# Output sums and two softplus steps on GpSimd in a selective scan, and a later issue of two small products in a mixture of experts

## The chip, the cores and the metric

One core of a Trainium2 chip runs the whole program in one launch. The metric is the device time in microseconds (us) of the program, as the median of several executions. The engines are TensorE (PE; its weight loads are PEld), VectorE (DVE), ScalarE (ACT), GpSimd (POOL) and SyncE (SP), which issues most DMAs. Each works through its own queue in order, and they wait for one another through semaphores.

## The reference, cut to what matters

The network has four layers on an image of 128 channels and 48 x 48 pixels, four images. Layer 0 is a selective scan in four directions, layer 1 a deformable convolution, layer 2 a linear attention and a mixture of experts, layer 3 a causal attention and a mixture of experts. The change is in layer 0 and in both mixtures. Of layer 0:

```python
xs = jnp.stack([x_hw, x_wh, x_hw[..., ::-1], x_wh[..., ::-1]], axis=1)
x_dbl = jnp.einsum('bkdl,kcd->bkcl', xs, x_proj_w)
dts, Bs, Cs = jnp.split(x_dbl, [R, R + N], axis=2)
delta = jax.nn.softplus(jnp.einsum('bkrl,kdr->bkdl', dts, dt_w) + dt_b[None, :, :, None])
A = -jnp.exp(A_logs)
out_y = _selective_scan(xs, delta, A, Bs, Cs, Ds)
inv = out_y[:, 2:4, :, ::-1]
y = out_y[:, 0] + inv[:, 0] + wh(out_y[:, 1]) + wh(inv[:, 1])
```

The scan is, for each channel and each of N = 16 states, h(t) = h(t-1) * exp(delta(t) * A) + delta(t) * u(t) * B(t), and the output is the sum over the states of h * C. Of the experts:

```python
logits = jnp.einsum('bsd,ed->bse', x, gate_w) + gate_b
probs = jax.nn.softmax(logits, axis=1)
vals, idx = jax.lax.top_k(probs.transpose(0, 2, 1), K)
```

where x is the layer-normed state: each of 64 experts takes its 8 best of 2304 tokens of an image, and its input is their sum, weighted by the probabilities.

## The kernel before, in words

**Layer 0** works on pieces. A piece is one image, one direction k and one third (768 positions, CH) of the sequence: 4 x 4 x 3 = 48 pieces, in the order of directions 0, 2, 1, 3 (PIECES). The 256 inner channels are two halves of 128 partitions, d = 0 and 1. A piece takes 16 steps, one for each state n, so there are 768 steps. What a step issues, and in which order, is written out by hand (STEPS, with a lag in steps for some parts):

```python
STEPS = """
pa s10 d1 s00 row t0 t2 fill t1 b0 e0 fill s11 s01 spread pb col b2 b1 fill e1 keep d0 fill
a2
"""
```

Every engine but SP takes its instructions in exactly this order. The parts: `pa` (times_b, L572) is POOL's product of du and B for the last 256 positions of both halves, one step ahead. `s10`, `s00`, `s11`, `s01` are the scans on DVE (L605), halves 1 and 0, first 512 positions and then 256; the first read their input b from PSUM, the second read what `pa` wrote in SBUF. `d0`, `d1` are exp(delta * A) on ACT (L557). `row` (L552) is a DMA on SP that spreads a row of B over the partitions for `pa`. `spread` (L539) is a select on POOL that lays column B out as diagonal blocks dB, three steps ahead, into two buffers; `e0`, `e1` (fill_b, L582) are PE's products of dB and du into the two PSUM banks b, one step ahead. `t0`, `t2`, `t1` transpose h on PE (L619), ACT scales by C (L629), `b0`, `b1` transpose back and sum in PSUM (L651); for the middle 256 positions `a2` sums on DVE instead (L643). `keep` (L612) saves the last state on POOL. So `spread` of a step waits for `e1` of the same step, which frees its buffer, and the next step's first scan waits for that `e1` too.

`col` is, in steps 3 and 4, `collect` of the piece before: for direction 0 it writes u * D + ys to y (L694, always on DVE), for the other three it adds ys to y (L703), for directions 1 and 3 with the two spatial axes exchanged. After the last one of an image, y goes to memory (SP), from where the tail of that image fetches it.

Each `fill` takes the next items of two lanes, spread evenly over the fills: the lane `next` prepares the next piece (31 items over 48 fills), the lane `image` does the tail of the image before or the head of the next. The items of `next` that matter are, in order: `log(0)`, `carry`, `less(0)`, `log(1)`, `total(0)`, `inputs(0)`, `less(1)`, `total(1)`, `inputs(1)`, and then the transposes of du on PE. They end the softplus, log(1 + e) + max(., 0), with a correction for rounding: `rest` (DVE, L459) finds the correction, `log` is ACT, `less` (L467) subtracts the correction from the logarithm, `total` (L470) adds that to delta, `inputs` (L474) multiplies delta and u into du. All are 128 x 768 for one half d.

**The experts** (`_experts`, once for layer 2 and once for layer 3) work on two pairs of images, q = 0 and 1. `shifted(b)` (L2091) makes -mean * rstd of image b on DVE, for all 18 token tiles at once; `gates(q)` normalises tokens (L2112 and L2110: one tile of three each on ACT, DVE and POOL), transposes them (L2127) and projects them on the experts (L2138); `select(q)` finds the eight largest of each expert on DVE (MAX8, L2160) and goes on from there. ACT's share of the normalising uses `shift`. The last of rstd of image 3 is a power on POOL, of layer 2's end (L1228) or of layer 3's (L2555). Then 16 groups of four experts are computed, whose weights SP loads into four buffers.

Of the kernel before, what the change touches and what calls it, by code (L numbers as in the profile page):

```python
# [24 lines left out]
NB = 4  # L25
# [102 lines left out]
def _layer0(ctx, env, dr, io, table, offs):  # L128
# [7 lines left out]
    nc, tc, ident = env.nc, env.tc, env.ident  # L136
# [255 lines left out]
    def prepare(x, before_it):  # L392

        k, at = x.k, x.at
        t = {}
# [68 lines left out]
            nc.scalar.activation(x.du[:, d, :], x.du[:, d, :], AF.Ln)  # L464

        def less(d):
            nc.vector.tensor_sub(x.du[:, d, :], x.du[:, d, :], t["e"][:, d, :])  # L467

        def total(d):
            nc.vector.tensor_add(x.delta[:, d, :], x.delta[:, d, :], x.du[:, d, :])  # L470

        def inputs(d):

# [17 lines left out]
        def carry():  # L491
# [23 lines left out]
            lambda: log(0),  # L515
            carry,
            lambda: less(0),
            lambda: log(1),
            lambda: total(0),
            lambda: inputs(0),  # L520
            lambda: less(1),
            lambda: total(1),
            lambda: inputs(1),
        ] + [
# [158 lines left out]
    def collect(x, d):  # L683

        src = x.ys[:, d, :]
        if x.k % 2:
            w0 = x.c * (CH // HW)
            dst = y[:, d, :].rearrange("p (h w) -> p w h", w=HW)
            dst = dst[:, w0 : w0 + CH // HW, :]
            src = src.rearrange("p (w h) -> p w h", h=HW)  # L690
        else:
            dst = y[:, d, x.at : x.at + CH]
        if x.k == 0:
            nc.vector.scalar_tensor_tensor(  # L694
                dst,
                u_hw[:, d, x.at : x.at + CH],
                dsum[:, d : d + 1],
                src,
                op0=ALU.mult,
                op1=ALU.add,  # L700
            )
        else:
            nc.vector.tensor_add(dst, dst, src)  # L703
        if (x.k, x.c, x.ci) == PIECES[-1] and d == ND - 1:
            nc.sync.dma_start(x.im.y, y)

# [271 lines left out]
    with tc.manual_schedule(engines=ORDERED):  # L978
# [20 lines left out]
        for g in range(len(pieces) * NS - min(lags.values())):  # L999
            i, n = divmod(g, NS)  # L1000
            b, p = divmod(i, NPI)
# [27 lines left out]
        for d in range(ND):  # L1029
            collect(pieces[-1], d)  # L1030
# [1014 lines left out]
def experts(env, io, pre, T, known, out=None):  # L2045


    with ExitStack() as ctx:
        _experts(ctx, env, io, pre, T, known, out)


def _experts(ctx, env, io, pre, T, known, final):


    nc, tc, ident = env.nc, env.tc, env.ident
# [7 lines left out]
    def psum(*shape):  # L2063
        return ps.tile(list(shape), F32, name="psum", tag="ps")
# [23 lines left out]
    def shifted(b):  # L2088
        mv, rstd = known[b]
        shift = sp.tile([P, NT], F32, name="shift", bufs=NB)  # L2090
        nc.vector.scalar_tensor_tensor(  # L2091
            shift, mv[:, :, 0], -1.0, rstd, op0=ALU.mult, op1=ALU.mult
        )
        image[b].update(mv=mv, rstd=rstd, shift=shift)

    def gates(q):

        t = {}

        def norm(j):  # L2100
            for r in range(2):
                b = 2 * q + r
                m = image[b]
                for g in range(G3):
                    i = j * G3 + g
                    src, dst = T[:, b * NT + i, :], xh[:, b * NT + i, :]
                    scale = m["rstd"][:, i : i + 1]
                    if g == 0:
                        shift = m["shift"][:, i : i + 1]
                        nc.scalar.activation(dst, src, AF.Identity, bias=shift, scale=scale)  # L2110
                        continue
                    (nc.vector if g == 1 else nc.gpsimd).tensor_scalar(  # L2112
                        dst,
                        src,
                        m["mv"][:, i, 0:1],
                        scale,
                        op0=ALU.subtract,
                        op1=ALU.mult,
                    )

        def turn(j):
            t[j] = []
            for r in range(2):
                pt = psum(P, BLK)
                for g in range(G3):
                    i = (2 * q + r) * NT + j * G3 + g
                    nc.tensor.transpose(pt[:, bass.ts(g, P)], xh[:, i, :], ident)  # L2127
                xT = sp.tile([P, BLK], F32, name=f"xT{r}")
                if r:
                    nc.scalar.copy(xT, pt)  # L2130
                else:
                    nc.vector.tensor_copy(xT, pt)
                t[j].append(xT)

        def project(j):
            pg = psum(P, BLK)
            for r, xT in enumerate(t.pop(j)):
                nc.tensor.matmul(  # L2138
                    pg[r * NE : (r + 1) * NE, :], gate_w, xT, start=True, stop=True
                )  # L2140
            nc.scalar.activation(G[:, q, bass.ts(j, BLK)], pg, AF.Identity, bias=gate_b)

        def step(j):
            if j + 1 < NBLK:
                norm(j + 1)
            if 0 <= j < NBLK:
                turn(j)
            if j > 0:
                project(j - 1)

        return [lambda j=j: step(j) for j in range(-1, NBLK + 1)]
# [120 lines left out]
    def turn_T(tT, n):  # L2272

        pt = psum(P, BLK)
        for g in range(G3):
            nc.tensor.transpose(pt[:, bass.ts(g, P)], T[:, n * G3 + g, :], ident)
        dst = tT[:, bass.ts(n, BLK)]
        if n % 2:
            nc.scalar.copy(dst, pt)
        else:  # L2280
            nc.vector.tensor_copy(dst, pt)

    def both(a, b):

        n = max(len(a), len(b))
        for i in range(n):
            for s in (a, b):
                for x in s[i * len(s) // n : (i + 1) * len(s) // n]:
                    x()

    with tc.manual_schedule(engines=ORDERED):
        for b in range(NB):
            shifted(b)
        both(gates(0), [])
        both(gates(1), select(0))
        both(select(1), [])
        tT = None
        if final is not None:
            tT = cp.tile([P, NB * L], F32, name="tT", tag="xh")
        last, turns = None, 0  # L2300
        for n in range(NE // EG + 1):
            new = Group(n * EG) if n < NE // EG else None
            if new:
                new.hidden()
            if last:
                last.output()
            if new:
                new.turned()
            if last:
                last.keep()  # L2310
            while tT is not None and turns * (NE // EG) < NB * NBLK * n:
                turn_T(tT, turns)
                turns += 1
            last = new
        for q in range(npair):
            pt = psum(P, C)
            both_oT = oT[:, 2 * q : 2 * q + 2, :].rearrange("p b e -> p (b e)")
            nc.tensor.transpose(pt, both_oT, ident)
            o = sp.tile([P, C], F32, name="o")
            nc.scalar.copy(o, pt)  # L2320

            halves = [slice(r * NE, (r + 1) * NE) for r in range(2)]
            for j in range(NBLK):
                pp = [psum(P, BLK) for r in range(2)]
                if final is None:
                    for g in range(G3):
                        for r, half in enumerate(halves):
                            nc.tensor.matmul(
                                pp[r][:, bass.ts(g, P)],
                                G[half, q, bass.ts(j * G3 + g, P)],  # L2330
                                o[half, :],
                                start=True,
                                stop=True,
                            )
                    for r in range(2):
                        i0 = (2 * q + r) * NT + j * G3
                        dst = T[:, i0 : i0 + G3, :].rearrange("p g c -> p (g c)")
                        nc.vector.tensor_add(dst, dst, pp[r])
                    continue
                for r, half in enumerate(halves):  # L2340
                    nc.tensor.matmul(
                        pp[r], o[half, :], G[half, q, bass.ts(j, BLK)], start=True, stop=True
                    )
                for r in range(2):
                    b = 2 * q + r
                    res = sp.tile([P, BLK], F32, name="res", tag=f"xT{r}")
                    nc.vector.tensor_add(res, tT[:, bass.ts(b * NBLK + j, BLK)], pp[r])
                    nc.sync.dma_start(final[b][:, bass.ts(j, BLK)], res)
# [516 lines left out]
```

## Time and profile before

| what | value |
|---|---|
| median of 3 runs | 10886.33 us (10877.05 to 10887.75) |
| the profiled execution | 10882.38 us |
| its span, first to last instruction | 10880.7 us |
| mean granted TensorE clock | 0.951 |
| layer 0, about | 145 to 4700 us of the span |
| deformable convolution, linear attention | 4700 to 9195 us |
| experts of layer 2 | 9195 to 9390 us |
| layer 3's attention | 9390 to 10707 us |
| experts of layer 3 | 10707 to 10880 us |

The page gives, for each engine, its busy time and share of the span, then costly groups of instructions: line, engine, operation, what is written and read, shape and count, then busy time in us, the mean of one in ns, and the engine's idle time just before them with what ended most of it. The timeline gives instructions in order: start and duration in us, engine, line, operation, and in brackets the idle time of the engine before it and what ended it. Neighbours of one kind are merged (x2), and one instruction's start can lie some 0.08 us before the end of the one ahead of it.

### The profile page before, as it was taken

Reading aid. Unit: us, or ns where it says so; the run is one execution under the profiler, and the core shown is the slowest. Engines: PE = TensorE matmul, PEld = TensorE weight load, DVE = VectorE, ACT = ScalarE, POOL = GpSimd, SP = SyncE. Lnnn points to the kernel's source line nnn. Section 1 sums busy time; section 2 is a strip of 40 time slices with the busy share of each in tenths; the row PEclk is TensorE's granted clock in tenths of the full one; section 3 lists DMA queues with packets and bytes.
Section 4 is the critical chain, followed back from the end, with each engine's and each line's share of the span. In section 5 each row is a group of like instructions: output and inputs, shape, how many; then the busy total and the mean of one; then the engine's idle time right before and its main releaser. Section 6 shows DMA issues by size and latency. Waiting matters only on the chain. (4 is left out here: it accounts for less than half of the span.)

```text
span 10880.7 us, 211759 instructions
## 1 busy us (share of the span) xinstructions
PE 9607.1 (88%) x82560; PEld 7581.2 (70%) x82560; DVE 8293.1 (76%) x15739; ACT 6673.8 (61%) x11320; POOL 4186.2 (38%) x4773
## 2 busy tenths in 40 slices
PE   7999889988998899857778999999999997799887
PEld 6789777977797777645666878877778875333333
DVE  5998899889988999755677888877888876455553
ACT  5777777777777777612234777767777775233333
POOL 2433343334333434356655444434444443000001
PEclk9999999999999999867888999999999999899999
DMA  4222223222322232255544000000000001200004
GB/s 138 75 81 70 81 83 97 70 77 85 96 73 79 83 92 76 86 175 166 155 138 121 27 25 27 28 21 26 25 27 27 24 28 50 98 7 8 8 9 145
DMA packets 424637, 763.45 MB, mean 70 GB/s; under 512 B 85428, under 2 KB 246983, under 8 KB 422487
## 3 DMA queue, kind: packets, MB, share of 16 engines
q1 hardware_dynamic: 368266, 576.68, 16.5%
q0 software_dynamic: 51840, 169.91, 5.5%
q8 instruction: 657, 10.76, 0.4%
q10 hardware_dynamic: 3532, 3.30, 0.1%
q14 instruction: 342, 2.79, 0.1%
HBM read 608.94 MB, written 74.69 MB: 63 GB/s over the span
## 5 line engine op out<-in xcount | busy, mean ns | idle before, releaser
L629 ACT ACTIVATE hs<-ps,bct 128x256 f32<-128x256 f32 x3072 | 1285.8, 473 | 775.5 <-PE yp L651 411.1
L582 PE MATMUL b<-dB,duT 128*128 128x128 f32 x12288 | 1694.9, 282 | 65.2 <-DVE h L605 53.5
L582 PEld LDWEIGHTS b<-dB,duT 128*128 128x128 f32 x12288 | 1531.0, 195 | 183.7 <-DVE h L605 79.5
L539 POOL TENSOR_SCALAR_AFFINE_SELECT dB<-bct 128x512 f32<-128x512 f32 x768 | 575.8, 750 | 2666.0 <-PE b L582 2569.4
L557 ACT ACTIVATE dA<-delta,l_Al 128x768 f32<-128x768 f32 x1536 | 1406.8, 939 | 161.5 <-DVE h L605 159.6
L619 PE MATMUL ps<-ident,h 128*128 128x128 f32 x9216 | 1249.8, 277 | 203.8 <-DVE acc L643 141.6
L605 DVE TENSOR_TENSOR_SCAN h<-dA,carry,b 128x512 f32<-128x512 f32 x1024 | 1252.7, 1264 | 218.8 <-PE b L582 187.8
L619 PEld LDWEIGHTS ps<-ident,h 128*128 128x128 f32 x9216 | 1033.8, 142 | 393.8 <-DVE acc L643 185.3
L605 DVE TENSOR_TENSOR_SCAN h<-dA,h 128x256 f32<-128x256 f32 x1536 | 1074.8, 741 | 0.0
L572 POOL TENSOR_TENSOR h<-du,rB 128x512 f32<-128x512 f32 x768 | 1003.3, 1306 | 49.0 <-DVE du L474 6.6
L651 PE MATMUL yp<-ident,hs 128*128 128x128 f32 x6144 | 950.8, 277 | 59.2 <-ACT hs L629 46.7
L2580 ACT ACTIVATE pT<-scT 128x768 f32<-128x768 f32 (+2 forms) x504 | 378.1, 750 | 728.4 <-PE scT L2572 728.3
L651 PEld LDWEIGHTS yp<-ident,hs 128*128 128x128 f32 x6144 | 728.9, 143 | 105.9 <-ACT hs L629 71.1
L605 DVE TENSOR_TENSOR_SCAN h<-dA,b 128x512 f32<-128x512 f32 x512 | 595.2, 1204 | 121.6 <-PE b L582 108.5
L1868 ACT ACTIVATE gl<-psum,l_cols 128x384 f32<-128x384 f32 x768 | 438.1, 581 | 317.6 <-PE psum L1867 288.4
L643 DVE SCALAR_TENSOR_TENSOR acc<-ps,bct,acc 128x256 f32<-128x256 f32 x1440 | 617.9, 470 | 1.5 <-PE ps L619 1.5
L1341 POOL DMA_INDIRECT g<-table,idx x476 | 520.7, 1094 | 252.2 <-issue 80.2
L1876 PEld LDWEIGHTS psum<-w,gl 128*128 128x128 f32 x4608 | 567.7, 193 | 50.1 <-ACT gl L1868 0.6
L1876 PE MATMUL psum<-w,gl 128*128 128x128 f32 x4608 | 594.5, 277 | 0.5 <-ACT gl L1868 0.5
L1867 PE MATMUL psum<-uT,w 128*128 128x384 f32 x1536 | 577.2, 498 | 0.8 <-ACT gl L1868 0.5
L1526 POOL TENSOR_TENSOR wk<-wk,wkr 128x384 f32<-128x384 f32 x171 | 172.2, 1007 | 1054.3 <-DVE wk L1525 1036.6
L2512 DVE TENSOR_REDUCE mx<-sc 128x4 f32<-128x2048 f32 (+2 forms) x200 | 396.6, 1983 | 213.8 <-PE sc L2501 211.1
(426 smaller groups left out, 20388.7 us busy)
## 6 DMA issues: line engine op xcount, KB each, us to landing
rB<-rows SPq DMA_DIRECT2D x768, 384.0 KB
w<-f_w SPq DMA_DIRECT2D x64, 1024.0 KB
wkr<-wk SPq DMA_DIRECT2D x384, 96.0 KB
wqr<-wq SPq DMA_DIRECT2D x384, 96.0 KB
table<-zero SPq DMA_DIRECT2D x162, 128.0 KB
table<-tok SPq DMA_DIRECT2D x16, 1152.0 KB
yd<-y SPq DMA_DIRECT2D x4, 2304.0 KB
sums<-raw SPq DMA_DIRECT2D x192, 48.0 KB
```

The costliest lines, as they stand in the source:

```text
L539: nc.gpsimd.affine_select(out=x.dB[n], in_=x.bc[:, m0 : m0 + CT // P, n : n + 1].to_broadcast([P, CT // P, P]), pattern=[[0, CT // P], [1, ...
L557: nc.scalar.activation(dA, x.delta[:, d, :], AF.Exp, scale=A[:, d, x.k, n : n + 1])
L572: engine.tensor_mul(h[:, :, lo:hi], x.du[:, :, lo:hi], rb)
L582: nc.tensor.matmul(bt[:, bass.ts(m, P)], x.duT[d][:, m, :], x.dB[n][:, m0 + m, :], start=True, stop=True,)
L605: nc.vector.tensor_tensor_scan(h, da, src, initial=first, op0=ALU.mult, op1=ALU.add)
L619: nc.tensor.transpose(tt[:, m, bass.ts(d, P)], x.h[n][:, d, bass.ts(2 * q + m, P)], ident)
L629: nc.scalar.activation(hs, tt[:, m, :], AF.Copy, scale=c)
L643: nc.vector.scalar_tensor_tensor(acc[:, m, :], tt[:, m, :], c, acc[:, m, :], op0=ALU.mult, op1=ALU.add)
L651: nc.tensor.matmul(yp[:, q, (2 * d + m) * P : (2 * d + m + 1) * P], hs[:, bass.ts(d, P)], ident, is_transpose=True, start=n == 0 and m == ...
L1341: nc.gpsimd.indirect_dma_start(out=g, out_offset=None, in_=table, in_offset=bass.IndirectOffsetOnAxis(ap=self.idx[:, k : k + 1], axis=0),)
L1867: nc.tensor.matmul(pg, y.w["w1"][:, bass.ts(f, P)], t["uT"], start=True, stop=True)
L1876: nc.tensor.matmul(pp[:, g, :], t["gl"][:, f, bass.ts(g, P)], y.w["w2"][:, f, :], start=f == 0, stop=f == DFF // P - 1,)
```

## The change

Three lines move from DVE to POOL, and one loop of the experts is split:

```diff
         def less(d):
-            nc.vector.tensor_sub(x.du[:, d, :], x.du[:, d, :], t["e"][:, d, :])
+            nc.gpsimd.tensor_sub(x.du[:, d, :], x.du[:, d, :], t["e"][:, d, :])

         def total(d):
-            nc.vector.tensor_add(x.delta[:, d, :], x.delta[:, d, :], x.du[:, d, :])
+            nc.gpsimd.tensor_add(x.delta[:, d, :], x.delta[:, d, :], x.du[:, d, :])
...
         else:
-            nc.vector.tensor_add(dst, dst, src)
+            nc.gpsimd.tensor_add(dst, dst, src)
...
     with tc.manual_schedule(engines=ORDERED):
-        for b in range(NB):
+        for b in range(2):
             shifted(b)
         both(gates(0), [])
+        for b in range(2, NB):
+            shifted(b)
         both(gates(1), select(0))
         both(select(1), [])
```

`less` and `total` are issued 96 times each, the addition of `collect` 72 times (three directions of four), all 128 x 768. Their places in the order of issue stay. `inputs`, between them on DVE, now reads what POOL wrote. In the experts, `shifted` of images 2 and 3 is issued behind the whole of `gates(0)`.

## The prediction

> **What bounds the kernel now.** I read the page first, then busy times by stretch, then the trace of layer 0 row by row, since 264 of the moved instructions lie there.
>
> From the page and from the busy times by stretch (span, then PE, PEld, DVE, ACT, POOL busy, clock, DMA share, GB/s):
>
> ```profile
> PE 9607.1 (88%) x82560; PEld 7581.2 (70%) x82560; DVE 8293.1 (76%) x15739; ACT 6673.8 (61%) x11320; POOL 4186.2 (38%) x4773
> ```
> ```profile
> 2500.00:3000.00 500.00, 447.80 (x3471) 386.58 (x3470) 465.16 (x680) 373.96 (x670) 203.03 (x242) 0.98 0.31 91
> 4700.00:9195.00 4495.00, 3998.31 (x41332) 3322.89 (x41333) 3372.99 (x8632) 2772.46 (x4461) 2229.78 (x2372) 0.94 0.20 61
> ```
>
> In layer 0 (about 145 to 4545 us) DVE and PE are both nine tenths busy and POOL four tenths: on averages, moving work from DVE to POOL looks free. So I cut the trace into steps, each beginning with the first of four scans (L605); 16 steps make a piece, 48 pieces the layer. A step without extra work takes 4.41 us, all of it DVE's: two long scans 2.36, two short ones 1.29, the two adds of L643 0.77. By the mean over pieces, steps 0 to 2 are PE's (DVE idles 0.8 to 1.5 us before the scans that follow) and steps 3 to 12 are DVE's (PE idles 0.65 us in step 8, 1.94 in step 9). In 35 of the 47 pieces prepared inside this loop `less(0)` stands in step 7, `total(0)` and `inputs(0)` side by side at the end of step 8, `less(1)` in the middle and `total(1)` at the end of step 9, `inputs(1)` in the middle of step 10; in 9 of the other 12 `total(0)` and `inputs(0)` stand side by side as well, later. Mean lengths of steps 7 to 10: 5.89, 6.47, 6.28, 5.64 us. Here is one step 8, DVE and then POOL (start, duration, idle time before it and who ended it):
>
> ```profile
> 1457.78 2.44 DVE L605 TENSOR_TENSOR_SCAN h<-dA,carry,b 128x512 f32<-128x512 f32 x2
> 1460.14 1.36 DVE L605 TENSOR_TENSOR_SCAN h<-dA,h 128x256 f32<-128x256 f32 x2
> 1461.43 0.93 DVE L470 TENSOR_TENSOR delta<-delta,du 128x768 f32<-128x768 f32 x1
> 1462.39 1.27 DVE L474 TENSOR_TENSOR du<-delta,u_hw 128x768 f32<-128x768 f32 x1
> 1463.59 0.86 DVE L643 SCALAR_TENSOR_TENSOR acc<-ps,bct,acc 128x256 f32<-128x256 f32 x2
> ```
> ```profile
> 1457.55 1.28 POOL L572 TENSOR_TENSOR h<-du,rB 128x512 f32<-128x512 f32 x1
> 1462.01 0.84 POOL L539 TENSOR_SCALAR_AFFINE_SELECT dB<-bct 128x512 f32<-128x512 f32 x1 [3.18 <-PE b L582]
> 1462.82 1.96 POOL L572 TENSOR_TENSOR h<-du,rB 128x512 f32<-128x512 f32 x1
> ```
>
> The reader is to see two things. POOL's `spread` (L539) waits for the last `fill_b` of PE in each step; over the pieces it starts 4.02 us (median) into step 8, when DVE is past its scans. Whatever POOL is given after `spread` starts no earlier. And two instructions that overlap get longer: the select took 0.84 instead of 0.64 while L470 ran, L474 1.27 instead of 0.95 while the select ran, L572 1.96 instead of 1.28 while L474 ran. Each waits about as long as the other still runs. It holds for short scans too (POOL, then DVE, which took 1.36 in the rows above):
>
> ```profile
> 1394.64 1.55 POOL L358 COPY u_wh<-u_hw 128x768 f32<-128x768 f32 x1
> ```
> ```profile
> 1395.02 2.36 DVE L605 TENSOR_TENSOR_SCAN h<-dA,h 128x256 f32<-128x256 f32 x2
> ```
>
> The long scans, which read b in PSUM, run at 2.44 beside L572 all through the layer. [...]
>
> **The change, step by step.** What DVE loses:
>
> ```profile
> L470 DVE TENSOR_TENSOR delta<-delta,du 128x768 f32<-128x768 f32 x96 | 100.3, 1045 | 0.4
> L703 DVE TENSOR_TENSOR y<-y,ys 128x768 f32<-128x768 f32 x72 | 96.1, 1336 | 3.6 <-ACT ys L678 3.6
> L467 DVE TENSOR_TENSOR du<-du,e 128x768 f32<-128x768 f32 x96 | 93.9, 978 | 0.0
> ```
>
> 290 us of DVE. POOL's price for 768 elements is not in the trace: it lies between 1.00 us for 384 (L1526) and 5.32 for 2304 (L1311); with 1.28 for 512 (L572) the line through the last two gives 1.28 + 256 x 2.25 ns = 1.86 us, which I take. The strided sums (two of three) may cost more: POOL's strided copy of 768 is 1.55, so I take 2.0. [...]
>
> *Step 7:* `less(0)` goes: -0.85 us (its start-to-start time; nothing, if PE bounds the step: the late tenth of `spread` is 6.29 there). On POOL it ends some 1.5 to 2 us into step 8, beside long scans; but the L572 behind it then meets the short scans, which the wait in step 8 hides.
>
> *Step 8:* `inputs(0)` on DVE now waits for `total(0)`, which stands behind `spread` in POOL's queue. 4.02 + 0.64 + 1.86 = 6.52 us. What POOL does next (`keep`, 0.26, in two pieces of three, else L572, 1.31: mean 0.61) has SBUF first: 7.13. Then `inputs(0)` 0.87 and L643 0.77: 8.77 us, against 6.47. +2.3. Without the 0.61 it is +1.7; with a `spread` at its late tenth (5.54) it is +3.2 or more. Behind `inputs(0)` on DVE stand L643 and the next scans, and PE waits for both.
>
> *Step 9:* `less(1)` and `total(1)` go: 6.28 - 0.85 - 0.95 = 4.48. But `spread` starts 4.66 us into step 9, so PE delivers no sooner; I take 4.8: -1.5 (bounds -1.8 and -1.0).
>
> *Step 10:* `total(1)` ends 4.66 + 0.64 + 1.86 = 7.16 us after the start of step 9, 2.36 into step 10, just when DVE comes to `inputs(1)`; the instruction behind it on POOL is first again (0.6) and an L572 then meets a short scan (0.3): +0.9 (bounds 0 and +1.3).
>
> Sum for a piece: -0.85 + 2.3 - 1.5 + 0.9 = +0.85; x 48 = **+41 us** (bounds -46 and +168: from -0.95 to +3.5 a piece, all of one side at once, which I don't expect).
>
> *Output sums:* 36 pieces, one each in steps 3 and 4. Step 3: DVE loses 1.26 of 5.96, but PE has 5.37 us of matmuls there at their usual spacing and `spread` starts at 4.94: -0.95. On POOL the sum then runs to 2.6 us into step 4 and L572 to 4.1, over the short scans due at 2.36: they lose 1.5, the second sum saves 1.26, +0.2. In step 5 L572 ends at 2.8: +0.4. Sum -0.35 x 36 = **-13 us** (bounds -91, both sums saved whole, and +22, nothing saved in step 3).
>
> *Ends of images:* PE waited 19.6 us in three times for y to come back (L729), DVE's last two sums take 2.84 us. Sums on POOL end 1.5 us later each time: **+5 us** (bounds 0 and +10). No SP queue is passed: y's DMA follows the same sum.
>
> *Experts.* `shifted` of images 2 and 3 goes behind `gates(0)`: two DVE instructions of 0.18 us, no DMA. In layer 2's experts the one for image 3 holds up DVE:
>
> ```profile
> 9214.71 12.47 POOL L2112 TENSOR_SCALAR xh<-T,known 128x128 f32<-128x128 f32 x16
> 9227.14 0.89 POOL L1228 TENSOR_TENSOR known<-known,half 128x3 f32<-128x3 f32 x1
> 9228.05 0.18 DVE L2091 SCALAR_TENSOR_TENSOR shift<-known 128x18 f32<-128x18 f32 x1 [17.43 <-POOL known L1228]
> ```
>
> Afterwards `gates(0)` (12.3 us long, 9228.05 to 9240.37) runs from 9210.6, its POOL part ready by 9219; the wait stays but comes behind it, so the first MAX8 can start at 9228.3 instead of 9240.37: **-12 us**, if POOL's order stays (bounds 0, if that square root slips behind, and -17.4). Weight loads follow the groups, which start as much earlier. In layer 3's experts the wait is 3.16 us, but POOL starts its normalising only after it: **-1 us** (bounds 0 and -3.2).
>
> Total 41 - 13 + 5 - 13 = **+20 us**. The profiled execution was 10882.4 us (span 10880.7), 4 below the median of the three runs, 10886.3; on the median, 10906.
>
> **Rivals.** *Faster:* POOL and DVE hinder each other less than assumed, so that step 8 costs +1.7, step 10 nothing: -0.65 a piece, -31; the sums bring -1.2 x 36 = -43; with -13 and +3, -84: 10802. For it: long scans and L643 are over half of a step and are not hindered. Against it: the overlaps above, and PE's load in steps 3 and 4. It decides where the contention costs under 0.2 us a moved instruction. *Much slower:* one mechanism, POOL's queue. DVE's delayed step lets PE start its chain late, `spread` slips, and `total` with it, in both halves: `inputs(1)` stalls about 1.3 us more. +2.2 a piece, +106, sums 0, +5 - 13: 10984. It decides once `spread` in step 9 begins over 5 us into it. For it: the late tenth of `spread` there is 6.61. Against it: PE is idle 1.94 us in that step. *The experts' edit does nothing* (POOL's square root slips with it): 10918.
>
> **Numbers.** Forecast case, 10865 to 10950: 0.48. Faster, 10780 to 10865: 0.28. Much slower, 10950 to 11030: 0.19. Experts void, near 10918: 0.05. The range 10815 to 10985 leaves out a third of the second and half of the third. Faster by over 0.2% (about what a measurement of this kernel can tell, 22 us: below 10865) 0.28; within it 0.24, the lower half of the forecast case; above 10908 0.48, its upper half, the third and the fourth.
>
> **What would show it.** Step 8 near 8.8 us, with L474 waiting for POOL L470 about 2.5 us, 40-odd times; L474 in step 10 with little wait; step 9 near 4.8; L605's short scans longer in the mean than 741 ns; L467 and L470 on POOL near 1.9 us. The first MAX8 of layer 2's experts 12 us nearer to the last adds of its layer. Wrong if DVE's wait before L474 is under 1 us, or if steps 3 and 4 lose their full 1.26.

## The result, and the profile after

Measured beside the kernel before, the changed kernel takes 10994.25 us (median of 4 runs, 10976.29 to 11003.36) against 10887.04 (4 runs, 10877.05 to 10891.32). The ratio is 1.0094, 95% interval 1.0081 to 1.0106: slower by 107 us. The forecast, 10906, had the sign right and a fifth of the size, and the time lies 9 us above the range.

The profiled execution took 10976.29 us, with a span of 10974.6: 94 us longer than before's. Cut at the same events, the two traces differ as follows:

| stretch | before, us | after, us | difference |
|---|---|---|---|
| up to the first scan | 145.6 | 149.0 | +3.4 |
| first scan to the last step of layer 0 | 4391.4 | 4488.4 | +97.0 |
| rest of layer 0, to the first gather | 158.2 | 161.4 | +3.2 |
| deformable convolution to the last T of layer 2 | 4513.5 | 4506.5 | -7.0 |
| last T to the first MAX8 of layer 2's experts | 31.7 | 19.7 | -12.0 |
| first MAX8 to layer 3's first | 1483.8 | 1494.9 | +11.1 |
| layer 3's first MAX8 to the end | 156.5 | 154.7 | -1.8 |

The loss is in layer 0. The -7.0 and the +11.1 lie where no instruction is changed but layer 3's two `shifted`; in the traces of the other kernels below the stretch of the +11.1 is 1486 to 1497 us long, with the experts' edit and without it, so that before's, the shortest of all, is the odd one. The page of after (busy times; then busy us, mean ns and idle time of three groups):

```profile
PE 9642.2 (88%) x82560; PEld 7622.3 (69%) x82560; DVE 8181.9 (75%) x15475; ACT 6667.7 (61%) x11320; POOL 4694.0 (43%) x5037
...
L605 DVE TENSOR_TENSOR_SCAN h<-dA,carry,b 128x512 f32<-128x512 f32 x1024 | 1252.2, 1263 | 266.2 <-PE b L582 232.4
...
L605 DVE TENSOR_TENSOR_SCAN h<-dA,h 128x256 f32<-128x256 f32 x1536 | 1195.2, 818 | 0.0
L572 POOL TENSOR_TENSOR h<-du,rB 128x512 f32<-128x512 f32 x768 | 1045.8, 1362 | 41.7 <-DVE du L474 0.9
```

DVE gave away 290 us of work, and its busy time fell by 111 only. The long scans kept their 1.26 us; the short ones, of which nothing was changed, went from 741 to 818 ns. The waits of after between 100 and 4700 us (us in total, times, longest) show the new one, and the growth of an old one, which was 296.3 us in 252 times before:

```profile
DVE h L605 <- PE b L582: 380.4, 300, 9.7
...
DVE du L474 <- POOL delta L470: 120.2, 55, 4.2
```

Going through DVE's time in layer 0 from start to start closes the account. Gone: `less` 85.5, `total` 94.6, output sums 86.8, together -267 us. Come: short scans +125, the wait ahead of L474 +114, waits ahead of the scans +77, L474 itself +21, other rows some +27. That makes +97.

Step 8 and the start of step 9 of one piece, whose step 8 is a long one (9.67 us; the median is 8.75 in the regular pieces, as the 35 whose `total(0)` and `inputs(0)` stand at the end of step 8 are called from here on). From the timeline of after, DVE and POOL:

```profile
1483.57 2.45 DVE L605 TENSOR_TENSOR_SCAN h<-dA,carry,b 128x512 f32<-128x512 f32 x2
...
1484.20 1.83 POOL L467 TENSOR_TENSOR du<-du,e 128x768 f32<-128x768 f32 x1
...
1485.94 2.34 DVE L605 TENSOR_TENSOR_SCAN h<-dA,h 128x256 f32<-128x256 f32 x2
1485.98 1.75 POOL L572 TENSOR_TENSOR h<-du,rB 128x512 f32<-128x512 f32 x1
...
1487.82 0.89 POOL L539 TENSOR_SCALAR_AFFINE_SELECT dB<-bct 128x512 f32<-128x512 f32 x1
...
1488.68 1.81 POOL L470 TENSOR_TENSOR delta<-delta,du 128x768 f32<-128x768 f32 x1
...
1490.45 1.27 POOL L572 TENSOR_TENSOR h<-du,rB 128x512 f32<-128x512 f32 x1
1490.53 2.00 DVE L474 TENSOR_TENSOR du<-delta,u_hw 128x768 f32<-128x768 f32 x1 [2.25 <-POOL delta L470]
```

All of the predicted step 8 is there. `less` has pushed L572 onto the short scans (2.34 instead of 1.36 us for the pair), `total` runs behind the select, L474 waits 2.25 us for it, and then takes 2.00 us instead of 0.95 beside L572, next in POOL's queue, which started 0.08 us before it. (Of the 55 instructions L474 that waited, 22 took 2.0 us or more and 29 took 0.96.) What I had not put into the sum comes next, on PE, in the same timeline:

```profile
1485.05 1.08 PE L582 MATMUL b<-dB,duT 128*128 128x128 f32 x8
...
1494.65 1.74 PE L582 MATMUL b<-dB,duT 128*128 128x128 f32 x8 [4.45 <-DVE h L605]
...
1497.04 1.71 PE L582 MATMUL b<-dB,duT 128*128 128x128 f32 x8
...
1498.82 0.64 POOL L539 TENSOR_SCALAR_AFFINE_SELECT dB<-bct 128x512 f32<-128x512 f32 x1 [4.63 <-PE b L582]
```

The eight products that take 1.08 us in step 8 take 1.74 and 1.71 in step 9, and `spread` starts 5.6 us into that step. Busy times of after by stretch (PE, PEld, DVE, ACT, POOL, granted clock, DMA share, GB/s) say why:

```profile
1490.30:1494.60 4.30, 0.00 (x0) 0.00 (x0) 4.07 (x5) 1.38 (x3) 3.89 (x3) 1.00 0.62 204
1494.60:1498.80 4.20, 4.15 (x22) 4.18 (x23) 3.78 (x7) 0.94 (x1) 0.00 (x0) 0.59 0.00 1
1498.80:1502.80 4.00, 4.00 (x39) 4.00 (x38) 2.49 (x3) 3.00 (x6) 3.98 (x4) 1.00 0.00 0
```

PE does nothing for 4.3 us: it waits for the first scan of step 9, which DVE's wait and the longer L474 have put off. In the 4.2 us after that the granted clock is 0.59, and PE gets through 22 matmuls where the next 4.0 us hold 39. Over the trace of before, the products following a gap in PE's starts of under 2.5 us are 0.11 us apart, those after a gap of 3 us or more 0.213 (one such run of products begins at 0.11 and turns), and between 2.5 and 3 us both occur, the shortest gap with slow products behind it being 2.65 us. In after the border is wider: gaps of 2.7 to 3.4 us ahead of step 9's products are followed by either spacing, and after every longer one the products are slow, at once or within the first eight. The granted clock falls to a half in step 9 of 13 pieces before and of 24 after. In the piece above it stays there for 3.41 us (1494.99 to 1498.40). In steps 9 such slow spacing costs some 0.49 us a piece before (mean over 48) and 0.83 after.

### The profile page after: what moved, and what is told of

Same layout as the page of the kernel before. It is cut to its first block, busy times and chain, and to the rows that moved or that the text cites. A ratio compares the mean times of both kernels' runs of the same rounds, so it can differ in the third digit from the quotient of the medians.

```text
span 10974.6 us, 211694 instructions
## 1 busy us (share of the span) xinstructions
PE 9642.2 (88%) x82560; PEld 7622.3 (69%) x82560; DVE 8181.9 (75%) x15475; ACT 6667.7 (61%) x11320; POOL 4694.0 (43%) x5037
## 5 line engine op out<-in xcount | busy, mean ns | idle before, releaser
L539 POOL TENSOR_SCALAR_AFFINE_SELECT dB<-bct 128x512 f32<-128x512 f32 x768 | 539.3, 702 | 2173.1 <-PE b L582 2168.9
L605 DVE TENSOR_TENSOR_SCAN h<-dA,carry,b 128x512 f32<-128x512 f32 x1024 | 1252.2, 1263 | 266.2 <-PE b L582 232.4
L605 DVE TENSOR_TENSOR_SCAN h<-dA,h 128x256 f32<-128x256 f32 x1536 | 1195.2, 818 | 0.0
L572 POOL TENSOR_TENSOR h<-du,rB 128x512 f32<-128x512 f32 x768 | 1045.8, 1362 | 41.7 <-DVE du L474 0.9
L643 DVE SCALAR_TENSOR_TENSOR acc<-ps,bct,acc 128x256 f32<-128x256 f32 x1440 | 614.2, 466 | 6.1 <-PE ps L619 6.1
```

The lines of the kernel that those rows point to most:

```text
L539: nc.gpsimd.affine_select(out=x.dB[n], in_=x.bc[:, m0 : m0 + CT // P, n : n + 1].to_broadcast([P, CT // P, P]), pattern=[[0, CT // P], [1, ...
L572: engine.tensor_mul(h[:, :, lo:hi], x.du[:, :, lo:hi], rb)
L605: nc.vector.tensor_tensor_scan(h, da, src, initial=first, op0=ALU.mult, op1=ALU.add)
L643: nc.vector.scalar_tensor_tensor(acc[:, m, :], tt[:, m, :], c, acc[:, m, :], op0=ALU.mult, op1=ALU.add)
```

## The experiments

Theories, made after the result. **W**: the loss comes from DVE's wait for `total(0)` behind `spread`, with what follows from it on PE. **P**: it comes from DVE and POOL excluding each other at SBUF, a guess from overlaps like that of L474 with L572 (2.00 us instead of 0.95), and the wait is a side matter. **C**, a part of W: PE's slow restart in step 9 (a clock of 0.59 in the piece above) is what step 9 lacks. Chips differ in the time of the kernel before (10746 to 10904 us, the difference lying behind layer 0), so each run has its ratio to before on its own chip. "Layer 0" below is the stretch from the first scan to the last step; before it is 4391.4 us, after 4488.4. It scatters by some 4 us: e3_experts, which changes nothing in layer 0, has 4395.6, and e14_after_again, which is the changed kernel once more, 4484.5.

**e1_softplus: before, with `less` and `total` on POOL**

```diff
-            nc.vector.tensor_sub(x.du[:, d, :], x.du[:, d, :], t["e"][:, d, :])
+            nc.gpsimd.tensor_sub(x.du[:, d, :], x.du[:, d, :], t["e"][:, d, :])
...
-            nc.vector.tensor_add(x.delta[:, d, :], x.delta[:, d, :], x.du[:, d, :])
+            nc.gpsimd.tensor_add(x.delta[:, d, :], x.delta[:, d, :], x.du[:, d, :])
```

> The kernel before with the softplus' subtraction and addition (less, total) alone on POOL; output sums stay on DVE, experts unchanged. The theory that the softplus part carries the loss (by the steps of the two traces: steps 7 to 14 got 2.1 us longer in sum, times 48 = 103, and the first piece's preparation 3): +95 to +115 us on before. Rival, that the output sums carry a good part of it through the delay of POOL's next products: +40 to +70 us here.

Measured: ratio 1.0102 (1.0085 to 1.0118), +105 us; layer 0 +103. The wait ahead of L474 is 122.9 us in 55 times, short scans are at 782 ns. The whole loss of layer 0 comes with these two lines.

**e2_sums: before, with the output sums on POOL**

```diff
-            nc.vector.tensor_add(dst, dst, src)
+            nc.gpsimd.tensor_add(dst, dst, src)
```

> The kernel before with the output sums of three directions alone on POOL. By the steps of the traces (steps 3 to 6: -0.70, -0.14, +0.60, +0.12 us, sum -0.12 a piece, plus 3 us at the end): -10 to +5 us. Rival, that the sums carry a good part of the loss: +30 to +60 us.

Measured: 1.0000 (0.9991 to 1.0010). DVE's 87 us of sums are gone from layer 0 and its short scans take 50 us more; steps 3 to 6 change by -0.72, -0.14, +0.61 and +0.10 us (means over the 48 pieces). What step 3 gains, step 5 gives back.

**e3_experts: before, with the later `shifted`**

```diff
-        for b in range(NB):
+        for b in range(2):
             shifted(b)
         both(gates(0), [])
+        for b in range(2, NB):
+            shifted(b)
```

> The kernel before with the experts' edit alone. If the wait for the last square root is taken out of the way of the first pair, as between the last sums of layer 2 and the first MAX8 in the trace after (22.2 us instead of 34.2): -10 to -16 us on before. Rival, that the weight loads or a lower clock in layer 3 take it back: within 4 us of before.

Measured: 0.9989 (0.9980 to 0.9999), -14 us. From the last T of layer 2 to the first MAX8 it is 19.0 us instead of 31.7.

**e4_apart: the changed kernel, with more between `total` and `inputs` of a half**

```diff
             lambda: total(0),
-            lambda: inputs(0),
             lambda: less(1),
+            lambda: inputs(0),
             lambda: total(1),
+            take_(turn, 0, 0, 4),
+            free_(turned, 0, 0, 4),
             lambda: inputs(1),
-        ] + [
...
+            take_(turn, 1, 0, 4),
+            free_(turned, 1, 0, 4),
         ]
```

> The changed kernel with the lane's items in another order: total(0), less(1), inputs(0), total(1), transposes of half 0, inputs(1), transposes of half 1, so that each product on DVE comes at least a third of a step later behind the total on POOL that it waits for. Theory W, that DVE's wait for total (120 us in the trace after) and what follows from it on PE carry the loss: DVE's wait before L474 falls under 25 us and the time to 10840 to 10910. Theory P, that POOL and DVE exclude each other from SBUF and so the moved work costs DVE nearly what it cost before: the wait falls, but the time stays between 10930 and 10990, with the short scans' mean still near 818 ns or above.

Measured: 0.9986 (0.9976 to 0.9995), -19 us against before; layer 0 4381.7, 107 us less than after, with the same additions on POOL. The waits of e4_apart between 100 and 4700 us:

```profile
DVE du L474 <- POOL delta L470: 30.7, 14, 4.2
```

The short scans are at 837 ns, longer than in after (818), and the kernel is faster all the same. P as the sole cause falls. With three quarters of the wait gone, longer short scans (+151 us) and longer L474 (+26) still take back two thirds of the 267 us that DVE gave away in layer 0, and layer 0 is 10 us shorter than before's.

**e5_contend: before, with an addition on POOL that nobody waits for, ahead of each `less` and `total`**

```diff
+        def spend(d):
+            i = pieces.index(x)
+            if i > 1:
+                nc.gpsimd.tensor_add(
+                    pieces[i - 2].ys[:, d, :],
...
         def less(d):
+            spend(d)
...
         def total(d):
+            spend(d)
```

> The kernel before, with 128x768 additions on POOL that nobody waits for added where less and total are issued (two constant operands, the output goes into a sums buffer that is not in use; they are no part of the computation). DVE's work is unchanged. This is POOL's and DVE's competition for SBUF by itself. Theory P, exclusion: the short scans' sum grows by 60 to 100 us and DVE's own less, total and inputs get longer too; time +60 to +130 us on before. Rival, that only waits cost: within 15 us of before.

Measured: 1.0172 (1.0155 to 1.0189), +186 us; layer 0 +198.5 for 184 additions, 1.08 us each. More than I expected. Groups of e5_contend between 100 and 4700 us (a helper shifts the line numbers: L481 is `total`, L477 `less`):

```profile
L469 POOL TENSOR_TENSOR ys<-inT 128x768 f32<-128x768 f32 x184 | 390.4, 2123 | 0.7
L481 DVE TENSOR_TENSOR delta<-delta,du 128x768 f32<-128x768 f32 x96 | 135.3, 1409 | 0.4
L477 DVE TENSOR_TENSOR du<-du,e 128x768 f32<-128x768 f32 x96 | 127.7, 1330 | 0.0
```

No instruction of DVE was added, and `total` went from 1045 to 1409 ns, `less` from 978 to 1330, and the short scans from 741 to 777; the long scans, whose b is in PSUM, stayed at 1263 (1264 before) and L643, which reads `ps` there, at 470.

**e6_write_only: the same, but POOL only writes**

```diff
+        def spend(d):
+            i = pieces.index(x)
+            if i > 1:
+                for n in (CH, CH, CH // 3):
+                    nc.gpsimd.memset(pieces[i - 2].ys[:, d, :n], 0.0)
```

> As e5_contend, but each added addition on POOL is three memsets of 768, 768 and 256 elements, of about the same time in sum (0.74 + 0.74 + 0.31 us by rows of the trace before), which write SBUF and read nothing; they are no part of the computation. e5_contend cost 1.7%, 198 us in layer 0. Theory P (what excludes DVE is that POOL reads SBUF while DVE has two operands there): the memsets themselves hinder nobody, only POOL's product comes later and meets the short scans: +10 to +70 us, DVE's less and total keep their old length. Rival Q, that POOL's busy time itself, by lateness of its product and select, was the cost: +120 to +200 us again.

Measured: 1.0029 (1.0020 to 1.0039), +33 us; layer 0 +29. DVE's `total` takes 6 us more in all, `less` 1, short scans 30. The memsets keep POOL busy for 328 us, e5's additions for 390. So of e5's +198.5 most comes with reading SBUF on POOL, not with POOL being taken: 198.5 us for additions that read it, 29 for memsets that only write.

**e7_select_last: the changed kernel, with `spread` at the end of a step, behind the fills**

```diff
-pa s10 d1 s00 row t0 t2 fill t1 b0 e0 fill s11 s01 spread pb col b2 b1 fill e1 keep d0 fill
-a2
+pa s10 d1 s00 row t0 t2 fill t1 b0 e0 fill s11 s01 pb col b2 b1 fill e1 keep d0 fill
+spread a2
```

> The changed kernel with POOL's select (spread) issued at the end of a step, behind the fills and keep; the lane's items stay in their order. If DVE's wait before L474 comes from total(0) standing behind the select in POOL's queue, the wait falls from 120 to under 40 us and the time to within 30 us of before (ratio 0.997 to 1.003). Rival, that total(0) on POOL is simply too slow for a product that is issued one place behind it: the wait stays over 80 us and the ratio over 1.005.

Measured: 0.9979 (0.9970 to 0.9989), -24 us; layer 0 4367.9, 120 us less than after. Only the select's place in the order differs from after. Waits of e7_select_last between 100 and 4700 us, and its short scans on the page:

```profile
DVE du L474 <- POOL delta L470: 22.7, 8, 4.1
```
```profile
L605 DVE TENSOR_TENSOR_SCAN h<-dA,h 128x256 f32<-128x256 f32 x1536 | 1259.6, 860 | 0.0
```

POOL's additions now run sooner and meet more short scans (860 ns), yet layer 0 is shorter than before's.

**e8_second_half: before, with `less` and `total` of half 1 alone on POOL**

```diff
-            nc.gpsimd.tensor_sub(x.du[:, d, :], x.du[:, d, :], t["e"][:, d, :])
+            (nc.gpsimd if d else nc.vector).tensor_sub(x.du[:, d, :], x.du[:, d, :], t["e"][:, d, :])
...
-            nc.gpsimd.tensor_add(x.delta[:, d, :], x.delta[:, d, :], x.du[:, d, :])
+            (nc.gpsimd if d else nc.vector).tensor_add(x.delta[:, d, :], x.delta[:, d, :], x.du[:, d, :])
```

(lines against after; the sums and the experts are as before.)

> The kernel before with less and total of half 1 alone on POOL; half 0 and the sums stay on DVE. The long wait was that of inputs(0); inputs(1) stands a third of a step behind total(1). Expected: wait before L474 under 30 us, 88 us taken off DVE, some 35 to 50 us given back by longer short scans: -30 to +5 us on before. Rival, that half 1's wait and PE's late chain in step 10 cost as much as half 0's: +20 to +60 us.

Measured: 1.0006 (0.9996 to 1.0017), +7 us, just outside what I expected, with an interval from -4 to +19. Step 9 falls by 0.84 us and step 10 rises by 0.97 (means over the 48 pieces); the wait is 18 us. It tells that half 0 makes the loss, not more.

**e9_sums_split: before, with the sums on POOL in halves, over steps 3 to 6**

```diff
-        src = x.ys[:, d, :]
+        own = CH // n
+        src = x.ys[:, d, i * own : (i + 1) * own]
...
+                        elif 3 <= n < 7:
+                            collect(x, (n - 3) // 2, (n - 3) % 2, 2)
```

> The kernel before with the output sums of three directions on POOL, but each cut in two and spread over steps 3 to 6 (an image's last piece stays whole, in steps 3 and 4). A step has about 3.1 us in which DVE reads at most one operand from SBUF (long scans and L643), and POOL's select, copy and product fill 2.2 of it. Theory P: half a sum (1.0 us) nearly fits, so the short scans grow by under 25 us instead of 50 and the time falls by 10 to 35 us. Rival, that PE bounds steps 3 and 4 and nothing can be had there: within 8 us of before, as with the whole sums.

Measured: 0.9993 (0.9983 to 1.0003); layer 0 -12. The short scans took 44 us more, against under 25 expected: smaller pieces do not pass between them unhindered. I had expected 10 to 35 us off the time; it does not separate a small gain from none.

**e10_last_apart, e11_last_softplus, e12_last_only: `spread` last, and more or less of the rest.** e10 is e7 with e4's order of the lane. e11 is e7 with the output sums on DVE. e12 is before with `spread` last and the experts' edit, and all three additions on DVE.

> The changed kernel with both cures: select at the end of a step and each product issued later behind its total. If the wait is what costs and the two cures add up, the remaining wait before L474 (17 us with the select last) goes: ratio 0.9955 to 0.9975. Rival, that the moved additions now meet more short scans and take the gain back: 0.9975 to 0.999, with the short scans' mean over 860 ns.

> The changed kernel with the select at the end of a step, but the output sums on DVE. The sums alone made no difference with the select in its old place. Expected: the same as with them, 0.997 to 0.999. Rival, that with the select last the sums gain on their own (step 4 fell by 0.45 us there): 0.999 to 1.002 without them.

> The kernel before with the select at the end of a step and the experts' edit; all of the additions stay on DVE. It tells whether what e7_select_last gained comes from the moved additions or from the select's place. If from the additions: 0.998 to 1.0 (the experts' 14 us alone are 0.9987). Rival, from the select's place: 0.9965 to 0.998.

| run | ratio (95%) | layer 0, us | wait ahead of L474, us | short scan, ns |
|---|---|---|---|---|
| e7 | 0.9979 (0.9970 to 0.9989) | 4367.9 | 22.7 | 860 |
| e10 | 0.9980 (0.9971 to 0.9989) | 4369.1 | 22.7 | 860 |
| e11 | 0.9994 (0.9985 to 1.0003) | 4390.1 | 22.4 | 819 |
| e12 | 0.9983 (0.9974 to 0.9992) | 4384.9 | none | 740 |

The two cures do not add up, as e10's rival had it: with the select out of the way the order of the lane is indifferent. e11 too lies in the range of its rival and not in mine, and e12, which I gave 0.998 to 1.0 if the additions made e7's gain and 0.9965 to 0.998 if the select's place did, lies at the border with an interval over both. e12 has e7's gain within the intervals, with nothing moved to POOL: 14 us of the experts (e3) and 6.5 us in layer 0 from the place of the select, little more than the scatter of 4 us. By layer 0's traces all moved additions together are worth 17 us on top of that (4384.9 to 4367.9), 2.7 of which go ahead of the first scan; the times resolve no difference between e7 and e12. `less` and `total` alone, in e11, are worth nothing (4390.1 against 4384.9), so what gain there is comes from the sums. The fastest versions run, e7 and e10, beat both kernels, by 0.2% against before.

**e13_warm and e14_after_again: PE kept busy through DVE's wait.** e13 is the changed kernel; in 32 pieces (not 36, as I had counted) PE repeats the four transposes `t1` of step 8's state six more times, 24 transposes more in each. My condition takes in 31 of the 35 regular pieces and misses four, which serve as a comparison within the same trace. e14 is the changed kernel itself, on the same chip.

```diff
-        for m in range(2):
+        warm = q == 1 and n == 8 and not 7 <= pieces.index(x) % 12 < 11
+        for m in [0, 1] * (7 if warm else 1):
```

> The changed kernel, in which PE repeats the eight-fold 128x128 transposes of one tile (t1) six more times in step 9 of the 36 pieces whose long wait lies in step 8: 24 transposes more, 2.6 us at their usual spacing, into the same place with the same result, where PE otherwise idles for over 4 us. Theory C: PE's products at the end of step 9 run at half rate after that idle (spacing 0.213 instead of 0.11 us) and so deliver late; busy PE keeps its clock: select of step 9 starts near 4.5 us into it instead of 5.5, step 9 gets 0.4 to 1.0 us shorter in these pieces, 15 to 35 us in all against the changed kernel. Rival: the lateness is only DVE's delay handed on: step 9 stays within 0.2 us, or gets longer by the added work.

> The changed kernel itself, beside e13_warm on one chip, so that the two can be compared: ratio to before 1.008 to 1.0106, as in the first comparison.

Measured: e13 1.0055 (1.0038 to 1.0072), e14 1.0079 (1.0062 to 1.0095), 28 us apart; layer 0 4453.0 and 4484.5. e14 lies just below the 1.008 that I expected at least. The timeline of e13_warm, PE, in the same piece as above:

```profile
1484.35 3.96 PE L620 MATMUL ps<-ident,h 128*128 128x128 f32 x32 [0.31 <-DVE h L605]
1488.15 0.60 PE L652 MATMUL yp<-ident,hs 128*128 128x128 f32 x4
1490.59 1.13 PE L582 MATMUL b<-dB,duT 128*128 128x128 f32 x8 [1.84 <-DVE h L605]
```

Its step 9, by the columns above (the clock stays at 1.00):

```profile
1489.18:1494.24 5.06, 3.44 (x28) 3.11 (x28) 5.06 (x9) 2.34 (x5) 2.07 (x3) 1.00 0.17 52
```

DVE's wait is nearly as long as in after (116.4 us in all, against 120.2), PE does more work, and the kernel is faster: the products now take 1.13 us where they took 1.74. `spread` in step 9 starts at 4.24 us instead of 5.50 (medians), slow spacing there falls from 0.93 us a piece to 0.21, and the step's change in regular pieces goes from -0.79 to -1.45 us. In e13's own trace it is -1.53 in the 31 pieces with the extra transposes and -0.84 in the four without; the granted clock falls in step 9 of two of the 31 and of three of the four. C holds.

## Why the prediction was wrong, point by point

For the 35 regular pieces, mean change of a step (us) against the terms of the sum:

| step | forecast | after | e13_warm |
|---|---|---|---|
| 7 | -0.85 | -0.86 | -0.87 |
| 8 | +2.3 | +2.07 | +2.06 |
| 9 | -1.5 | -0.73 | -1.45 |
| 10 | +0.9 | +1.34 | +1.13 |
| 11 to 15 | none | +0.18 | +0.05 |

**Steps 7 and 8 were right**, in mechanism and size: 42 waits of L474 in the first half's places, 2.25 us in the median, and a median step of 8.75 against 8.77. But the forecast laid the places of the 35 regular pieces over lengths that are means of all 48: in the 35, step 8 took 6.88 us before, not 6.47, and step 9 took 6.78, not 6.28. L470 takes 1.82 us on POOL (put at 1.86), a strided sum 2.24 (put at 2.0). The 0.61 us for what POOL does next were an estimate from lengths and overlaps in before's trace. In after L474 takes 0.96 us where no instruction of POOL runs at its start (29 of the 55 that waited), 1.37 beside a select (4), 2.00 beside L572 (18) and 2.54 beside L467 (4); over the 42 it takes 0.48 us more than 0.96 in the mean.

**Step 9 is the step that failed.** The text has it: "`spread` starts 4.66 us into step 9, so PE delivers no sooner; I take 4.8". That took the place of `spread` over from before, as if the stall in step 8 could not touch it. But DVE's wait, with the longer L474 behind it, leaves PE without work, in the piece above for over 4 us; PE comes back at a clock of 0.59, and `spread` starts at 5.52 (medians of all pieces). In the regular pieces step 9 takes 6.05 us instead of 4.8, and the wait ahead of the scans at its end grows from 0.12 us a piece to 1.23. The much slower rival began with this condition ("once `spread` in step 9 begins over 5 us into it") and had the place right; it put the cause down to a late start of PE's chain and not to its speed, and its price on `inputs(1)`. e13_warm shows that the clock makes most of this: with the clock kept up, and DVE's wait for `total(0)` left as it is, the wait ahead of the scans is 0.49 us and step 9 gives -1.45. That it meets -1.5 so closely is luck: it also removes slow spacing that before had there (0.49 us a piece), and from 6.78 a step of 4.8 would have been -1.98. The step takes 5.33 us in e13_warm; what holds the half microsecond above 4.8 was not looked for. Price: 0.77 x 35 = 27 us.

**Step 10 was mis-sized**: +1.34 for +0.9, 15 us. The term that was too small is that of the short scans: they take 0.88 us longer there, put at 0.3. L474 takes 0.39 longer (0.6 put) and waits in 3 of the 35 pieces only (4.4 us in all), as forecast; the piece above is one of them, where it waits 1.46 us and then takes 2.00.

**The 12 irregular pieces were the other failing step.** I charged them the regular +0.85 from seeing that `total(0)` and `inputs(0)` stand side by side there too, "later". They cost 2.69 us each: there the additions fall into steps 11 to 13 (+0.96, +1.18, +0.64) and every one of these steps gets longer; none gives anything back. L474 waits there for both halves, 41 us in all, 3.4 a piece. 1.84 x 12 = 22 us. Together with 6 us in steps 11 to 15 and 8 us less in step 8, this makes 27 + 15 + 22 + 6 - 8 = 62 us, the gap between the +41 of the forecast and the +103 of e1_softplus.

**Output sums** were put at -13 us in the steps. For such a piece the terms -0.95, +0.2 and +0.4 make -0.71, +0.15 and +0.3 in the mean of all 48; e2_sums has -0.72, -0.14, +0.61 and, in step 6, +0.10. Step 3 was right, step 4 came out better and step 5, where the second sum's L572 meets the short scans, at twice its price: -0.15 x 48 = -7 us, and other steps took that back (-0.7 us in all of layer 0's steps).

**Ends of images** were right: PE waits 24.4 us in three times for y to come back, 19.6 before (+5 put). **Experts**: -13 put, -14 in e3_experts. The first MAX8 still waits for image 3's `shift`, but by 7.14 us instead of 17.43 (DVE in the timeline of after):

```profile
9324.90 0.18 DVE L2091 SCALAR_TENSOR_TENSOR shift<-known 128x18 f32<-128x18 f32 x1 [7.14 <-POOL known L1228]
9325.00 2.55 DVE L2160 MAX8 top<-G 128x8 f32<-128x2304 f32 x1
```

**Not in the forecast**: the first piece's preparation, ahead of the first scan, has nothing to hide behind; with four additions on POOL it takes 3.4 us more (4.5 in e1_softplus; 1.7 in e3_experts, where nothing is changed in it, so that part of this is scatter).

**Open**: the medians lie 107 us apart and the profiled executions 94; on another chip the same kernel, e14, is 86 us over before, and e1, e2 and e3 add up to 91. How much of the 107 is scatter is not settled. Nor is what makes layer 3's attention 11.1 us shorter in before's trace than in after's.

## What to carry to other kernels

An instruction moved to an engine with idle time starts when that engine's queue lets it: look for an instruction that waits at the queue's head (here a select, 2169 us of waiting in all) ahead of a result that another engine needs at once; moving either of the two took 107 and 120 us off layer 0, where the change had cost 97. A stall on one engine of a pipeline has to be followed to the others: here gaps of 2.65 us and more in PE's starts were followed, not every time, by products 0.213 us apart instead of 0.11, and step 9 lost 0.83 us a piece to such spacing, against 0.49 before the change. And work moved from DVE to POOL was no gain by itself here: 290 us moved brought nothing that the times could show even where the wait was down to 23 us (e7 against e12).

## What the hardware showed that I had not expected

An addition on POOL that nobody needs costs layer 0 more than DVE's own addition would: 1.08 us for each of 184 in e5_contend, against the 0.94 (85.5 + 94.6 us over 192 in all) that `less` and `total` occupy DVE in before. And more PE work made the kernel faster: in e13_warm the extra transposes, which nobody needs, bring 28 us.
